# Joining the output products of two head groups, folding the value bias away, a rotary step with one addition, and new engine orders

## The chip, the cores and the metric

The kernel runs on one core of a Trainium2 chip. The core has a matrix engine (TensorE, here PE, with its weight loads shown apart as PEld), a vector engine (DVE), a scalar engine (ACT), a general engine (GpSimd, here POOL), and a queue (SyncE, here SP) that issues DMAs. They work side by side and wait for one another through semaphores; each engine takes its own instructions in the order in which the program gives them. The metric is the device time of one execution in microseconds, the median of the runs.

## The reference

Sixteen sequences of 256 tokens and 256 features go through two layers; the input of every layer step is added back to its output.

```python
x = x + attn0(cond_a(x, fside))       # cross-attention to fside, then 16 causal heads of 16 with rotary
x = x + ffn0(cond_b(x))               # matmul with a weight chosen per sequence, then FP4-quantized gated FFN
x = x + attn1(diffuse(x))             # Laplacian step, RMS norm, 16 heads of 64 in segments of 128, 16 memory tokens
x = x + moe(cond_c(x))                # gelu MLP with a chosen expert, then 8 experts, the best 2 per token
```

What the change touches in it:

```python
qkv = x @ w_qkv.T + b_qkv                         # attn0: the last third of b_qkv is the value bias
out = einsum('bhts,bhsd->bhtd', probs, v)         # rows of probs sum to 1
return out @ w_out.T + b_out
...
q = q * cos + _rotate_half(q) * sin               # attn1: rotary, k likewise
...
out = out.transpose(0, 2, 1, 3).reshape(b * w, SEG, HEADS * dh)
out = out @ W_out                                 # attn1: one product over all 16 heads
```

Everything is float32.

## The kernel before

The program has two parts. The first, `woven` (L367), does the first three lines of the reference for all sequences; the second, `mixture` (L1340), does the last. Only a little of the second (`stage_c`, L596) is pulled into the first.

In the first part the work is written as 19 stages. Each is a Python generator (`stage_a`, `stage_h`, ...) that yields one engine instruction at a time, or a condition that must hold before it goes on. The planner `weave` (L215) holds the next instruction of every stage, reckons from a table of costs (L123 to L134, `Unit.cost`) when each could start on its engine, and emits the one with the earliest start. Among those of the same engine that could start within `SLACK` of it, the rank of the stage in `ORDER` (L135) decides. So the order on each engine, SP's DMA queue included, is fixed when the program is built, by planned times and not by those of the chip. When PE's next planned start lies over `GAP` behind its last end, the planner may put in a product of the identity with itself (`kept_warm`, L394), if that fits with a `MARGIN` of 0.2 us:

```python
if best is not None and best[2][0] == "PE" and best[2][2] and best[3] > free.get("PE", 0.0) + GAP:
    op = spare()
    ...
        if max(at, ready(op, "PE")) + c[1] + MARGIN < best[3]:
```

PSUM, into which PE writes, is cut into two pairs of banks and four single banks, which the stages take in turn. Nearly every instruction of this part is recorded under L186, the line of the helper that makes it, so the profile's groups are told apart by the names of tiles.

The stages that matter here:

- `stage_a` (L439) loads the weights of the first attention (`wqkv0`, `bqkv0`, `bout0`, `wout0`) and then, for each sequence, loads `x`, adds `bout0` to it on POOL and projects queries, keys and values (`project_heads`, L663). There the biases are added on DVE, that of the values in one instruction per half sequence, `b_v<-pair,bqkv`.
- `stage_gate`, `stage_up` and `stage_down` quantize the weights of the feed-forward step at the start.
- `stage_p` and `stage_k` make queries and keys of the second attention, in 4 groups of 4 heads for each sequence, 64 groups in all. `turned4` (L1193) multiplies the projected halves by the cosines (`f_t1q`, `f_t1k`) and by the sines (`f_t2q`, `f_t2k`) on DVE, combines them by two additions on POOL, and moves the result to the layout of the scores by four DMAs (`f_q<-f_t1q`, `keys<-f_t1k`).
- `stage_s` makes the scores, `stage_g` (L1225) the exponentials. `stage_g` also issues the load of the group's 256 KB of output weights, `wo`, into one of two tiles.
- `stage_v` (L1241) calls `values4` (L1291) for each group: it transposes the probabilities (`f_prob` to `f_pT`), multiplies by the values, copies the result to `f_oT`, multiplies that by `wo` and adds the product to `x[b]` on DVE. In odd groups the memory tokens' part (`f_ppT` with `pmo`) joins the product's accumulation.

Of the kernel before, what the change touches and what calls it, by code (L numbers as in the profile page):

```python
# [13 lines left out]
F32 = mybir.dt.float32  # L14
# [97 lines left out]
class Op:  # L112
# [14 lines left out]
SIDE = {32: 0.125, 64: 0.2}  # L127
TURN = 0.01
XBUFS = 7
GAP = 0.6  # L130
MARGIN = 0.2
SLACK = {"PE": 0.0, "DVE": 0.05, "ACT": 0.1, "POOL": 0.02, "SP": 0.0}
EARLY = 200.0, 0.2
EASE = 1.5  # L134
ORDER = {  # L135
    "PE": "h y down a i m f s e g v d p gate c k x u up",
    "DVE": "d v f c h i x e a g k up gate p down u s m y",
    "ACT": "f p up h i k y gate m e a v d u g x c s down",
    "POOL": "m f h i e a y v down x g s d u up gate k p c",
    "SP": "v x a h i f p g s m d gate y u up k e c down",  # L140
}
BANK_LATER = {"PE": None, "DVE": True, "ACT": True, "POOL": None, "SP": None}


def is_ap(x):
# [293 lines left out]
def stage_a(g):  # L439
    k, a = g.k, g.a  # L440
    yield lambda: g.done["R"] == 3
    g.wqkv, op = load(g, g.w, "wqkv0", [P, 2, 3 * D], a["w_qkv0"])
    yield op
    g.bqkv, op = load(g, g.w, "bqkv0", [P, 3 * D], a["L0_attn_b_qkv"].unsqueeze(0).to_broadcast([P, 3 * D]))
    yield op
    for name in ("cos0", "sin0", "nsin0"):
        t, op = load(g, g.w, name, [P, 2, DH0 // 2], a[name])
        setattr(g, name, t)
        yield op
    g.bout, op = load(g, g.w, "bout0", [P, D], a["L0_attn_b_out"].unsqueeze(0).to_broadcast([P, D]))  # L450
    yield op
    g.wout0, op = load(g, g.w, "wout0", [P, 2, D], a["w_out0"])
    yield op


    g.done["I"] = 1
    for b in range(g.B):
        yield lambda: b < g.done["L"] + XBUFS
        x = g.x[b] = g.xp.tile([P, 2, D], F32, name="x", tag="x")
        yield g.sp.dma_start(out=x, in_=a["x"][b].rearrange("(p c) d -> p c d", p=P))  # L460
        yield lambda: g.done["B"] > b
        if b == 0:
            hT = g.first
            yield from head_constants(g)
        else:
            hT = g.a_.tile([P, 2, S], F32, name="a_h", tag="a_h", bufs=2)
            yield g.sp.dma_start(out=hT, in_=k.hd[b])
        yield g.pool.tensor_tensor(x, x, g.bout.unsqueeze(1).to_broadcast([P, 2, D]), ALU.add)
        yield lambda: g.done["M"] >= 2 * b and g.done["A"] >= b - 1
        yield from project_heads(g, b, hT)  # L470
        g.done["J"] = b + 1
# [11 lines left out]
def ahead(g, which):  # L483
# [9 lines left out]
    for b in range(which, g.B, 2):  # L493
# [7 lines left out]
        if b == 0:  # L501
            g.done["B"] += 1
            yield lambda: g.done["I"]
        else:
            yield g.sp.dma_start(out=g.k.hd[b], in_=own["e"])
            yield lambda: g.done["B"] == b
            g.done["B"] += 1


def head_constants(g):  # L510
# [152 lines left out]
def project_heads(g, b, hT):  # L663
# [4 lines left out]
    for st in range(2):  # L668
# [3 lines left out]
        yield from mm_(g, pq[:, 1, :D], [(hT[:, c, tok], g.wqkv[:, c, 2 * D : 3 * D]) for c in range(2)])  # L672
        qk = tile_a(g, 2 * D, "b_raw")
        yield g.dve.tensor_tensor(qk, pq[:, 0, :], g.bqkv[:, 0 : 2 * D], ALU.add)
        yield g.dve.tensor_tensor(v[:, st, :], pq[:, 1, :D], g.bqkv[:, 2 * D : 3 * D], ALU.add)
        g.pairs.append(pq)


# [345 lines left out]
def stage_p(g):  # L1024
# [22 lines left out]
    yield op  # L1047
    g.cos1, op = load(g, g.w, "cos1", [P, S], a["cos1"])
    yield op
    g.sin1, op = load(g, g.w, "sin1", [P, S], a["sin1"])  # L1050
    yield op

    g.pmo = g.w.tile([P, 2, D], F32, name="pmo")
    pmv = tile_l(g, [P, 2, 2, 2 * P], "wq", 2)
# [138 lines left out]
def turned4(g, zT, w, name, scale, move):  # L1193
# [3 lines left out]
    for r in range(2):  # L1197
        yield from mm_(g, pq[:, r, :], [(w[:, c, r * P : (r + 1) * P], zT[:, c, :]) for c in range(2)])
    t1, t2 = tile_l(g, [P, 2, S], f"f_t1{name}"), tile_l(g, [P, 2, S], f"f_t2{name}")
    for t, by in ((t1, g.cos1), (t2, g.sin1)):  # L1200
        table = by.unsqueeze(1).to_broadcast([P, 2, S])
        if scale is None:
            yield g.dve.tensor_tensor(t, pq, table, ALU.mult)
        else:
            yield g.dve.scalar_tensor_tensor(t, pq, scale, table, ALU.mult, ALU.mult)
    g.singles.append(one)
    yield g.pool.tensor_tensor(t1[:, 0, :], t1[:, 0, :], t2[:, 1, :], ALU.subtract)
    yield g.pool.tensor_tensor(t1[:, 1, :], t1[:, 1, :], t2[:, 0, :], ALU.add)
    for a in range(2):
        for r in range(2):  # L1210
            yield move(slice(r, P, 2), a, t1[64 * a : 64 * a + 64, r, :])
# [13 lines left out]
def stage_g(g):  # L1225

    for i in range(4 * g.B):
        yield lambda: (i, 0) in g.scored and g.done["V"] > i - 2
        wo = tile_l(g, [P, 2, D], "wo", 2)
        yield g.sp.dma_start(out=wo, in_=g.a["w_out1"][:, 2 * (i % 4) : 2 * (i % 4) + 2, :])  # L1230
        if i % 2 == 0:
            g.pm = tile_l(g, [P, 2, 8, PM], "f_pm", 2)
        prob = [None, None]
        g.live[i] = prob, g.pm, wo
        for st in range(2):
            yield lambda: (i, st) in g.scored
            prob[st] = yield from exponentials4(g, i % 4, st, *g.scored.pop((i, st)))
# [50 lines left out]
    return prob  # L1288


def values4(g, n, b, v, prob, pm, wo):  # L1291

    pT = []
    for st in range(2):
        yield lambda: g.done["G"] > 2 * (4 * b + n) + st
# [17 lines left out]
    oT = tile_l(g, [P, 2, S], "f_oT", 2)  # L1313
    yield copy_(g, twined(oT), untwined(po))
    g.singles.append(one)
    if n % 2 == 1:
        ppT = tile_l(g, [P, S], "f_ppT")
        one = yield from single(g, pm)
        pt = one[:, :S]
        for st in range(2):  # L1320
            yield g.pe.transpose(pt[:, st * P : (st + 1) * P], pm[:, st].rearrange("p j n -> p (j n)"), g.ident)
        rows = lambda t: t.unsqueeze(1)
        yield copy_(g, twined(rows(ppT)), untwined(rows(pt)))
        g.singles.append(one)
    one = yield from single(g, oT)
    pp = one.rearrange("p (s d) -> p s d", s=2)
    for st in range(2):
        tok = slice(st * P, (st + 1) * P)
        pairs = [(oT[:, c, tok], wo[:, c, :]) for c in range(2)]
        if n % 2 == 1:  # L1330
            pairs.append((ppT[:, tok], g.pmo[:, n // 2, :]))
        yield from mm_(g, pp[:, st, :], pairs)
    yield g.dve.tensor_tensor(g.x[b], g.x[b], pp, ALU.add)
    g.singles.append(one)
# [509 lines left out]
```

## Time and profile before

| | |
|---|---|
| runs | 2491.32 us median of 3 (2489.93 to 2493.8) |
| profiled execution | 2491.22 us, of which span 2489.5 us |
| planner-ordered part | about 0 to 1516 us of the span |
| expert part | about 1516 us to the end |
| granted PE clock, mean | 0.999 |
| PE busy | 2447.2 us, 98% |
| DVE, ACT, POOL busy | 1345.4, 1205.1, 1061.1 us |

The profile is one execution. Times are counted from the first instruction. A group line names engine, operation, the tile written and the tiles read, the shape (partitions x elements) and the count; then the busy time in us, the mean duration of one in ns, and the idle time of the engine before these instructions with what ended it. A PE line begins with the rows and columns of the stationary operand. A float32 product appears as two PE records; a transpose as one. A waits line says who waited for whom, in total us, how often, and the longest.

### The profile page before, as it was taken

The page shows a single profiled execution, that of the slowest core. Times are in us where ns is not written, and L with a number is a line of the kernel's source. Part 1 is how long each engine was busy: PE and PEld are TensorE (multiplying, and loading weights), DVE is VectorE, ACT ScalarE, POOL GpSimd, SP SyncE. Part 2 cuts the span into 40 slices and gives each one's busy share as a digit, 9 for nine tenths or more (in the row PEclk, how much of TensorE's full clock was granted, in tenths as well). Part 3 has the DMA queues.
Part 4 walks back from the last instruction along what each step waited for, and adds up shares of the span by engine and source line. Part 5 has one row for each costly group of instructions (what it writes and reads, how often), then busy time and mean ns, then how long its engine had stood idle before and what let it go on. Part 6 is the DMA issues. An engine that isn't in the chain of part 4 may idle for free. (4 is left out here: it accounts for less than half of the span.)

```text
span 2489.5 us, 39426 instructions
## 1 busy us (share of the span) xinstructions
PE 2447.2 (98%) x13339; PEld 1859.7 (75%) x13339; DVE 1345.4 (54%) x2640; ACT 1205.1 (48%) x3567; POOL 1061.1 (43%) x1212
## 2 busy tenths in 40 slices
PE   8999999999999999999999999999999999999999
PEld 7776777777777777777778885555668888888866
DVE  6777877978888877888876652333300000000023
ACT  3765666666676666666664554223212322322311
POOL 6555666666666656675665442333200000000044
PEclk9999999999999999999999999999999999999999
DMA  5432332322233232222233544111224556555433
GB/s 163 145 128 80 96 103 68 100 92 73 87 93 99 73 96 83 79 88 88 83 100 118 174 136 141 51 51 51 79 81 153 198 181 201 199 185 198 155 101 108
DMA packets 229725, 285.00 MB, mean 114 GB/s; under 512 B 45233, under 2 KB 192657, under 8 KB 220177
## 3 DMA queue, kind: packets, MB, share of 16 engines
q1 hardware_dynamic: 223376, 265.66, 33.7%
q0 software_dynamic: 6144, 16.79, 2.1%
q8 instruction: 108, 1.77, 0.3%
q14 instruction: 97, 0.79, 0.1%
HBM read 210.78 MB, written 33.82 MB: 98 GB/s over the span
## 5 line engine op out<-in xcount | busy, mean ns | idle before, releaser
L1472 POOL DMA_INDIRECT got<-osort,pos_o x64 | 62.0, 968 | 628.5 <-ACT hT L1405 585.6
L1454 ACT ACTIVATE ehT<-bank,own_b 128x256 f32<-128x256 f32 x280 | 132.5, 473 | 349.1 <-PE bank L53 349.1
L53 PE MATMUL bank<-ysT,w 128*128 128x256 f32 x1120 | 247.5, 379 | 0.2 <-ACT ysT L108 0.2
L53 PE MATMUL bank<-w,ehT 128*128 128x256 f32 x1120 | 247.5, 379 | 0.0
L186 PE MATMUL single<-e_zT,wq 128*128 128x256 f32 x1024 | 243.6, 381 | 1.8 <-DMA wq<-in_w_qk 1.0
L53 PEld LDWEIGHTS bank<-ysT,w 128*128 128x128 f32 x1120 | 212.7, 190 | 29.4 <-ACT ysT L108 0.5
L53 PEld LDWEIGHTS bank<-w,ehT 128*128 128x128 f32 x1120 | 210.2, 190 | 27.2
L186 POOL TENSOR_TENSOR b_e<-b_e,b_stat 128x1024 f32<-128x1024 f32 x124 | 186.1, 1502 | 104.2 <-DVE b_stat L186 87.4
L186 ACT ACTIVATE b_e<-b_e,b_stat 128x256 f32<-128x256 f32 x496 | 220.4, 448 | 12.8 <-DVE b_stat L186 12.7
L186 ACT ACTIVATE f_prob<-f_prob,f_stat 128x144 f32<-128x144 f32 x512 | 207.6, 409 | 24.7 <-DVE f_stat L186 24.5
L186 PEld LDWEIGHTS single<-e_zT,wq 128*128 128x128 f32 x1024 | 185.7, 190 | 26.4 <-issue 2.0
L186 POOL TENSOR_TENSOR f_prob<-f_prob,f_stat 128x512 f32<-128x512 f32 x128 | 136.1, 1063 | 110.6 <-DVE f_stat L186 98.3
L1462 DVE TENSOR_TENSOR eo<-bank,eb 128x512 f32<-128x512 f32 x35 | 24.2, 692 | 234.4 <-PE bank L53 234.4
L186 ACT COPY b_pT<-single 128x512 f32<-128x512 f32 x186 | 108.2, 586 | 68.2 <-PE single L186 67.6
L1569 POOL DMA_INDIRECT ysort<-r_y,r_posi x64 | 62.4, 976 | 162.9 <-DMA ysort<-r_y,r_posi 101.7
L186 PE MATMUL single<-wo,f_oT 128*128 128x256 f32 x512 | 128.2, 383 | 0.5 <-ACT f_oT L186 0.4
L1421 DVE COPY own_b<-b1t 128x8 f32<-128x8 f32 x35 | 5.9, 174 | 222.3 <-ACT ehT L1454 222.3
L186 PE MATMUL single<-wv,e_zT 128*128 128x256 f32 x512 | 121.9, 381 | 0.0
L1405 ACT ACTIVATE hT<-bank,b 128x512 f32<-128x512 f32 x64 | 43.9, 687 | 157.4 <-PE bank L53 151.2
L186 POOL TENSOR_TENSOR f_t1q<-f_t1q,f_t2q 128x256 f32<-128x256 f32 x128 | 99.3, 791 | 41.6 <-DVE f_t2q L186 20.4
L186 PE MATMUL single<-ident,b_e 128*128 128x128 f32 x744 | 113.0, 277 | 3.4 <-POOL b_e L186 1.2
L186 DVE TENSOR_REDUCE b_stat<-b_e 128x4 f32<-128x1024 f32 (+1 forms) x124 | 114.5, 941 | 1.4 <-ACT b_e L186 0.8
(329 smaller groups left out, 5406.4 us busy)
## 6 DMA issues: line engine op xcount, KB each, us to landing
w<-in_w SPq DMA_DIRECT2D x70, 1024.0 KB
wq<-in_w_qk SPq DMA_DIRECT2D x128, 256.0 KB
wv<-in_w_v SPq DMA_DIRECT2D x64, 256.0 KB
keys<-f_t1k SPq DMA_DIRECT2D x256, 64.0 KB
f_q<-f_t1q SPq DMA_DIRECT2D x256, 64.0 KB
wo<-in_w_out SPq DMA_DIRECT2D x64, 256.0 KB
ys<-ysort SPq DMA_DIRECT2D x35, 256.0 KB
osort<-eo SPq DMA_DIRECT2D x35, 256.0 KB
```

What stands on the lines that cost most here:

```text
L53: nc.tensor.matmul(out, lhsT, rhs, start=start and i == 0, stop=stop and i == last)
L186: return Op([(self.name, self.cost(fn, outs, aps), lambda: call(*args, **kw))], outs, aps)
L1405: nc.scalar.activation(hT[:, f, :], ph, AF.Gelu_apprx_tanh, bias=k.b1[:, NE, f : f + 1])
L1421: nc.vector.tensor_copy(b1, r.b1t[:, t, :])
L1454: nc.scalar.activation(hT[:, f, :], ph, AF.Gelu_apprx_tanh, bias=b1[:, f : f + 1])
L1462: nc.vector.tensor_tensor(o, po, b2.unsqueeze(1).to_broadcast([P, 2, D]), ALU.add)
L1472: nc.gpsimd.indirect_dma_start(out=g, out_offset=None, in_=k.osort[:, :], in_offset=bass.IndirectOffsetOnAxis(ap=r.pos_o[:, i, t : t + 1], ...
L1569: nc.gpsimd.indirect_dma_start(out=k.ysort[:, :], out_offset=bass.IndirectOffsetOnAxis(ap=posi[:, i, t : t + 1], axis=0), in_=ys[t], in_of ...
```

## The change

Four things are done at once.

- Output products: `values4` now issues the load of `wo` itself, at its head. An even group stops after `f_oT` and keeps `f_oT` and `wo`; the odd group that follows multiplies both groups' in one accumulation, with the memory tokens' part, and one addition to `x[b]` serves two groups.
- Value bias: a new function `output_bias` is called once in `stage_a` before the loop over sequences. It transposes the value bias, multiplies it by `wout0` and adds the product to `bout0`; this is the same sum, since the rows of the probabilities add up to 1. The values are copied out of PSUM by `copy_`, which lets the planner choose ACT or DVE.
- Rotary: the table of sines gets two rows, the first negated on POOL once; DVE reads the two halves in PSUM in swapped order, and a single POOL addition over 512 elements takes the place of two over 256.
- Orders: the ranks in `ORDER` are other ones for all five engines, and `GAP` is 0.3 in place of 0.6. `BANK_LATER` for PE becomes `True`; no PE instruction reads PSUM, so the term that it switches stays zero.

```diff
-GAP = 0.6
+GAP = 0.3
...
-    "PE": "h y down a i m f s e g v d p gate c k x u up",
-    "DVE": "d v f c h i x e a g k up gate p down u s m y",
-    "ACT": "f p up h i k y gate m e a v d u g x c s down",
-    "POOL": "m f h i e a y v down x g s d u up gate k p c",
-    "SP": "v x a h i f p g s m d gate y u up k e c down",
+    "PE": "h y down g a m i f s e v d gate p k u c x up",
+    "DVE": "d x v f c h i e a g k up gate down p s u m y",
+    "ACT": "up f p k h i y gate m e a d u v g c x s down",
+    "POOL": "e m f h i a y v down x g s d u up gate k p c",
+    "SP": "v x a h i g f p s m gate y u d up k e c down",
...
+    yield from output_bias(g)
     for b in range(g.B):
...
+def output_bias(g):
+    t = g.a_.tile([P, 2, P], F32, name="bvT", tag="b_raw")
+    one = yield from single(g, g.bqkv)
+    pt = one.rearrange("p (c t) -> p c t", t=P)
+    for c in range(2):
+        yield g.pe.transpose(pt[:, c, :], g.bqkv[:, 2 * D + c * P : 2 * D + (c + 1) * P], g.ident)
+    yield copy_(g, t, pt[:, :2, :])
+    g.singles.append(one)
+    one = yield from single(g, t)
+    yield from mm_(g, one[:, :D], [(t[:, c, :], g.wout0[:, c, :]) for c in range(2)])
+    yield g.dve.tensor_tensor(g.bout, g.bout, one[:, :D], ALU.add)
+    g.singles.append(one)
...
-        yield g.dve.tensor_tensor(v[:, st, :], pq[:, 1, :D], g.bqkv[:, 2 * D : 3 * D], ALU.add)
+        yield copy_(g, v[:, st, :], pq[:, 1, :D])
...
-    g.sin1, op = load(g, g.w, "sin1", [P, S], a["sin1"])
-    yield op
+    g.sin2 = g.w.tile([P, 2, S], F32, name="sin2")
+    yield g.sp.dma_start(out=g.sin2[:, 1, :], in_=a["sin1"])
+    yield g.pool.tensor_scalar(g.sin2[:, 0, :], g.sin2[:, 1, :], -1.0, None, ALU.mult)
...
-    for t, by in ((t1, g.cos1), (t2, g.sin1)):
-        table = by.unsqueeze(1).to_broadcast([P, 2, S])
+    for t, by, src in ((t1, g.cos1.unsqueeze(1).to_broadcast([P, 2, S]), pq), (t2, g.sin2, pq[:, ::-1, :])):
...
-    yield g.pool.tensor_tensor(t1[:, 0, :], t1[:, 0, :], t2[:, 1, :], ALU.subtract)
-    yield g.pool.tensor_tensor(t1[:, 1, :], t1[:, 1, :], t2[:, 0, :], ALU.add)
+    yield g.pool.tensor_tensor(t1, t1, t2, ALU.add)
...
-        wo = tile_l(g, [P, 2, D], "wo", 2)
-        yield g.sp.dma_start(out=wo, in_=g.a["w_out1"][:, 2 * (i % 4) : 2 * (i % 4) + 2, :])
...
-def values4(g, n, b, v, prob, pm, wo):
+def values4(g, n, b, v, prob, pm):
+    wo = tile_l(g, [P, 2, D], "wo", 2)
+    yield g.sp.dma_start(out=wo, in_=g.a["w_out1"][:, 2 * n : 2 * n + 2, :])
...
+    if n % 2 == 0:
+        g.even = oT, wo
+        return
...
-        pairs = [(oT[:, c, tok], wo[:, c, :]) for c in range(2)]
-        if n % 2 == 1:
-            pairs.append((ppT[:, tok], g.pmo[:, n // 2, :]))
+        pairs = [(o[:, c, tok], w[:, c, :]) for o, w in (g.even, (oT, wo)) for c in range(2)]
+        pairs.append((ppT[:, tok], g.pmo[:, n // 2, :]))
         yield from mm_(g, pp[:, st, :], pairs)
```

## The prediction

> **What bounds the kernel now.** I read the page's engine totals first, then busy time by stretch, then the groups of TensorE (PE) in a stretch, then what PE waited for, and last the rows of the operations that are edited.
>
> ```profile
> span 2489.5 us, 39426 instructions
> PE 2447.2 (98%) x13339; PEld 1859.7 (75%) x13339; DVE 1345.4 (54%) x2640; ACT 1205.1 (48%) x3567; POOL 1061.1 (43%) x1212
> PEclk9999999999999999999999999999999999999999
> ```
>
> PE is busy 98% of the span at full clock, no other engine above 54%. The profiled execution took 2491.22 us, 1.7 us around a span of 2489.5; the median of the runs is 2491.32. I sum against 2491.2.
>
> The planner-ordered part ends at about 1516 us, where the code of `mixture`, which the change leaves alone, begins. So I cut the span at 300, 1350 and 1516 us. Columns: stretch, its length, busy time of PE, weight loads, DVE, ACT, POOL, then clock and DMA.
>
> ```profile
> 0.00:300.00 300.00, 282.09 (x1720) 217.95 (x1721) 222.73 (x403) 175.02 (x547) 169.05 (x186) 1.00 0.39 123
> 300.00:1350.00 1050.00, 1038.17 (x6525) 781.03 (x6524) 844.92 (x1472) 683.98 (x2257) 673.03 (x764) 1.00 0.30 89
> 1350.00:1516.00 166.00, 164.10 (x1072) 132.86 (x1071) 88.99 (x160) 86.30 (x293) 74.35 (x111) 1.00 0.44 131
> 1516.00:2489.00 973.00, 962.79 (x4027) 727.82 (x4025) 188.81 (x610) 259.82 (x470) 144.66 (x152) 1.00 0.41 136
> ```
>
> PE idles 17.9 us in the first stretch, 11.8 in the second, 1.9 in the third. Busy PE is not all useful: the planner fills expected gaps with products of the identity with itself (`kept_warm`). They are the group that reads the identity alone; here for 0 to 300 us, then 300 to 1350, then 1350 to 1520.
>
> ```profile
> L186 PE MATMUL single<-ident 128*128 128x128 f32 x368 | 50.2, 284 | 1.7 <-POOL ident masks.py:199 1.6 <-DVE f_t2k L186 0.2
> ...
> L186 PE MATMUL single<-ident 128*128 128x128 f32 x4 | 1.0, 326 | 0.0
> ...
> L186 PE MATMUL single<-ident 128*128 128x128 f32 x28 | 4.6, 293 | 0.0
> ```
>
> So what can be won is 17.9 + 50.2 = 68 us at the start, 11.8 + 1.0 = 13 in the middle and 1.9 + 4.6 = 6.5 near its end, 87 us in all. The rest is PE at work, which the change does not shorten. In the middle PE waits in small pieces, for chains through POOL, DVE and ACT:
>
> ```profile
> PE single L186 <- POOL d_h L186: 1.7, 4, 0.6
> PE pair L186 <- POOL b_diag L186: 1.3, 4, 0.4
> PE single L186 <- DVE x L186: 1.2, 1, 1.2
> PE single L186 <- POOL b_qk L186: 1.1, 1, 1.1
> ```
>
> **The change part by part.** These rows price it (count, busy us, mean ns):
>
> ```profile
> L186 DVE TENSOR_TENSOR x<-x,single 128x512 f32<-128x512 f32 x80 | 54.4, 680 | 47.9 <-PE single L186 47.4
> L186 DVE TENSOR_TENSOR b_v<-pair,bqkv 128x256 f32<-128x256 f32 x32 | 13.1, 410 | 0.0
> L186 ACT COPY f_ppT<-single 128x256 f32<-128x256 f32 x32 | 12.0, 375 | 6.9 <-PE single L186 6.8
> L186 POOL TENSOR_TENSOR f_t1q<-f_t1q,f_t2q 128x256 f32<-128x256 f32 x128 | 99.3, 791 | 41.6 <-DVE f_t2q L186 20.4 <-DVE f_stat L186 12.1 <-issue 7.3
> L186 POOL TENSOR_TENSOR b_qk<-b_t,b_t 128x512 f32<-128x512 f32 x32 | 41.0, 1283 | 37.9 <-DVE b_t L186 26.4 <-DVE f_stat L186 9.3 <-DVE b_stat L186 1.5
> L186 POOL TENSOR_TENSOR f_prob<-f_prob,f_stat 128x512 f32<-128x512 f32 x128 | 136.1, 1063 | 110.6 <-DVE f_stat L186 98.3 <-PE single L186 10.9 <-DVE b_stat L186 0.3
> ```
>
> Output products. Two groups now add up in one PSUM bank. The products stay the same in number and size; 32 of the 80 additions to `x` go: 32 x 0.680 = 21.8 us of DVE, and 32 bank holdings. All of it lies beside PE.
>
> Value bias. 32 additions (13.1 us of DVE) become copies, which the planner may give to ACT at 0.375 each, 12 us there. Once, at the start: two transposes, a copy, two products and one addition to `bout0`. Transposes start 0.109 us apart and 256-wide records 0.216 apart, two records to a float32 product, so PE gets 2 x 0.109 + 4 x 0.216 = 1.1 us. It falls among the identity products after 13 us, so 0 on PE. If that cover is gone, 1.1. Its addition of 0.41 and perhaps its copy join a DVE that works on the weights' chain from 18 to 26 us, and PE waits 2.1 us for that chain at 23 us: between 0 and 1.1 us, I take 0.5. Behind it in its stage stand the load of `x[0]`, the constants on POOL (23.0 us) and the first projection (24.2). The loads before and with `wout0` add up to 3.35 MB, at the 226 GB/s of the first 25 us some 15 us after the first at 2.7. So the bias is done near 20 us, my estimate, and they do not wait.
>
> Rotary step. Two POOL additions of 0.79 (1.58 together) become one of 128x512, which the trace has not in this place: between 1.06 (`f_prob`, one operand a broadcast) and 1.33 (`x` + `bout`). I take 1.28 from `b_qk`, likewise two full tiles. 128 x 0.30 = 38 us of POOL, beside PE; the sine table's negation takes some 0.8 back, once. DVE reads the PSUM halves swapped and a two-row table, as many elements as before: 0.68 stays, at worst 0.83 as for the SBUF row `e_near` (128 x 0.15 = 19 us of DVE); I take 0. The moves of the first half could start after the first addition (at 1125.10, when POOL had begun at 1124.35); now all four wait 1.28 instead of 0.79, so SP's queue behind them is held 0.5 us longer per step. PE waits for none of these DMAs in the trace, so 0; with that cover gone it would be 128 x 0.5 = 64 us.
>
> Output weights. Their DMA, 64 times, moves from the softmax stage to the head of `values4`, so it leaves that place in SP's queue and stands ahead of the group's transposes instead. An even group's weights are needed a group later; their tile, one of two, is free once the odd product before has read it, so SP's queue, with the moves of `q` and `k` behind, can stand there for PE, as it did when the load sat in the softmax stage. An odd group's must land between its first transposes and its product.
>
> ```profile
> SPq L186 <- POOL f_t1q L186: 225.5, 74, 12.5
> SPq L186 <- POOL f_t1k L186: 213.3, 67, 13.1
> ```
>
> In SP's own waits, the queue stands for POOL up to 13.1 us, 3 us on average. The first weights were issued at 231.4 us for a product at 266.6. From first transposes to first product of an odd group I count, by start times in the timeline, 5.4 us at least and 14.5 in the median. A 256 KB load at 89 GB/s (the middle's mean rate, so a lower bound of speed) takes 2.9 us; with 3 us of queue it fits, with 13 it does not. I take 0; the range holds +1 us for each of 32 groups.
>
> The Trainium skill ("DMA: Bandwidth & Descriptors", Rules for kernel authors) says to issue a DMA early and wait for it late, which speaks against this move. By its fixed 2.0 us (Anatomy of one DMA, given for the gpsimd path) I estimate the load at some 5 us instead of 2.9, which still fits the median; no wait here shows the figure.
>
> Orders and gap. Every engine's order is set anew, and the identity product is now put in from gaps of 0.416 us (its planned 0.216 plus the margin of 0.2) instead of 0.6. PE's clock is 1.00 in every stretch already, and its longest wait for a releaser is 2.2 us, so more filling cannot raise the clock. One product costs 0.22 us where the gap was not there; with 184 now (368 records), 20 to 60 more cost 0 to 13 us if all missed, and I take 0 as they sit where PE would wait.
>
> The skill ("TensorE: Matmul & The Clock Gate", Why this matters for your kernels) asks only that no gap exceeds some 3 us. Agreed by the 2.2 us above; by that rule the smaller gap is worth nothing and can only cost.
>
> What the order is worth no row shows. It can move only the 87 us. At the start much is latency: the first loads, the weights' quantization, the first attention; 37 of the 50 us of filling lie before 110 us. I bound it there by a third won (-23) and by 15 us lost, and take -5. Relief on DVE and POOL adds -2 there, near 200 to 300 us where rotary begins. In the middle DVE loses 24 x 0.68 + 24 x 0.41 = 26 us of 845, POOL 96 x 0.30 = 29 of 673; of the 13 us of PE's loss I take a third, -4 (0 to -6). Near the end -1 (0 to -3).
>
> Sum: +0.5 - 5 - 2 - 4 - 1 = -11.5, so 2491.2 - 11.5 = 2479.7, say 2480. The ends of the likeliest case: -31 (2460) and -5 (2486).
>
> **The rivals.** (A) Hidden anyway: the start is bound by loads and chains that no order moves, and PE's small waits return behind other producers. For it: DVE and POOL are not the bound anywhere (80% and 64% in the middle). Against: 50 us of filling say that PE was short of ready work. Time 2486 to 2496. (B) Slower, by the order alone: priorities fitted to the planner's durations put a PE instruction ahead whose input comes later on the chip than planned, and PE takes its instructions in turn. Place: the first 300 us, where PE waits some 2 us for POOL's weights twice already. Ten such waits of 2 us cost 20, 2511; it decides once they exceed the 11.5 won, so from six on. Against: in the middle PE idles 1.1%, so plan and chip agree well. (C) Slower, by late output weights: 32 x 1 us = +32, less 11.5, so 2512; it decides where the average hold passes 0.36 us.
>
> **How the numbers follow.** Forecast 0.60, A 0.16, B 0.19, C 0.05. About 5 us (0.2%) is what a measurement tells from no change: faster 0.60, same 0.16, slower 0.24. The time is the likeliest case's, whose own range is 2460 to 2486. Over all cases 2460 to 2504 leaves out about 0.05 below and 0.13 above (the worse half of B and C).
>
> **What would show it.** Right: `x` additions of 512 fall from 80 to 48, no `b_v` addition, 128 POOL rotary additions near 1.28 us instead of 256; the stretch to 1516 ends about 12 us earlier, mostly by fewer identity products and less idle before 300 us; the part after it keeps 973 us. Wrong: PE waiting for DMA of the output weights (C), identity products or PE idle before 300 us above 68 us together (B), or POOL's addition above 1.58 us.

## The result and the profile after

The change made the kernel slower: 2525.7 us in the median (2522.71 to 2527.54) against 2492.56 us for the kernel before on the same chip, a ratio of 1.0131 with a 95% interval of 1.0114 to 1.0149. The prediction was 2480 us with a range of 2460 to 2504, so it had the wrong direction and the time lies outside its range. The profiled execution took 2527.54 us, with a span of 2525.8 us. The ratios here and below are those of fast runs; one execution of `edits_only`, 7186.29 us, was none and stands only in that run's median.

The engine totals of the page of after:

```profile
span 2525.8 us, 39290 instructions
PE 2474.4 (98%) x13463; PEld 1881.7 (74%) x13463; DVE 1325.2 (52%) x2578; ACT 1214.1 (48%) x3599; POOL 1032.1 (41%) x1085
```

DVE has 20.2 us less to do than before and POOL 29.0 less, and still the span is 36.3 us longer. PE looks as busy as it was, 98%, and is busy 27 us longer.

The busy time by stretch, after, with the columns of the prediction (stretch, its length, PE, weight loads, DVE, ACT, POOL, clock, DMA). The last product of the planner-ordered part ended at 1524.2 us before and ends at 1561.9 us now, so I cut there:

```profile
0.00:300.00 300.00, 288.43 (x1762) 225.71 (x1764) 209.52 (x377) 170.96 (x530) 163.31 (x170) 0.99 0.38 120
300.00:1350.00 1050.00, 1022.74 (x6380) 766.10 (x6379) 811.45 (x1393) 680.50 (x2264) 631.79 (x652) 0.99 0.30 87
1350.00:1561.90 211.90, 210.37 (x1318) 166.12 (x1316) 116.71 (x204) 105.10 (x343) 93.65 (x128) 1.00 0.42 123
```

All of the loss is in the ordered part: 1561.9 - 1524.2 = 37.7 us, while what follows takes 964 us, where it took 965. PE idles 11.6 us up to 300 us, where it was 17.9, but 27.3 us in the middle, where it was 11.8, and the clock is 0.99 in both stretches, where it was 1.00. The identity products of after, in 0 to 300, 300 to 1350 and 1350 to 1562 us:

```profile
L186 PE MATMUL single<-ident 128*128 128x128 f32 x466 | 63.2, 285 | 2.0 <-POOL ident masks.py:199 1.6 <-DVE b_pT L186 0.2 <-ACT e_zT L186 0.2
...
L186 PE MATMUL single<-ident 128*128 128x128 f32 x4 | 0.6, 274 | 0.0
...
L186 PE MATMUL single<-ident 128*128 128x128 f32 x48 | 7.3, 286 | 0.0
```

They take 71.1 us where they took 55.8. That gives a balance of the 37.7 us: 15.3 more of identity products, 8.8 more of idle time (11.6 + 27.3 + 1.5 = 40.4 against 17.9 + 11.8 + 1.9 = 31.6), some 1.1 for the products of the value bias, and at most 8.5 lost to the clock, which is worked out below; at least 4 us are not placed. The first 300 us have little of it: identity products and idle time come to 74.8 us there, where they were 68.1.

The edited operations, after:

```profile
L186 DVE TENSOR_TENSOR x<-x,single 128x512 f32<-128x512 f32 x48 | 32.7, 681 | 51.4 <-PE single L186 51.4
...
L186 ACT COPY b_v<-pair 128x256 f32<-128x256 f32 x32 | 11.9, 373 | 43.8 <-DVE b_raw L186 43.8
...
L186 POOL TENSOR_TENSOR f_t1q<-f_t1q,f_t2q 128x512 f32<-128x512 f32 x64 | 85.6, 1337 | 47.1 <-DVE f_stat L186 18.8 <-DVE f_t2q L186 14.9 <-issue 5.9
L186 POOL TENSOR_TENSOR f_t1k<-f_t1k,f_t2k 128x512 f32<-128x512 f32 x64 | 84.2, 1316 | 47.7 <-DVE f_t2k L186 22.6 <-DVE f_stat L186 12.4 <-issue 11.9
```

Each edit did to its own operations what it was expected to do. The time went elsewhere, and three places can be looked at.

**The start.** PE's timeline, after: the transposes of the value bias, its products with `wout0`, and the first projection of the first attention.

```profile
24.97 0.38 PE L186 MATMUL single<-ident,bqkv 128*128 128x128 f32 x2
...
26.75 1.03 PE L186 MATMUL single<-wout,bvT 128*128 128x256 f32 x4
...
40.59 1.88 PE L186 MATMUL pair<-wqkv,a_h 128*128 128x512 f32 x4
```

The same projection in PE's timeline of before:

```profile
24.16 1.88 PE L186 MATMUL pair<-wqkv,a_h 128*128 128x512 f32 x4
```

The load of `x[0]` in SP's timeline of before:

```profile
13.42 0.43 SPq L186 DMA_DIRECT2D x<-in_x  x1
```

The same load in SP's timeline of after:

```profile
27.01 0.43 SPq L186 DMA_DIRECT2D x<-in_x  x1
```

The bias was done only at 28 us. What stands behind it in `stage_a` waited for it: the load of `x[0]` by 13.6 us, the first projection by 16.4. How much PE lost by it is another matter. The 6.7 us that the first 300 us lost are no measure of it: `orders_only` below, which has no bias, has 59.9 us of identity products and 13.8 us of idle time there, 5.6 us more than before. The first product with `wo` begins at 304.3 us instead of 266.6, but the joined products put it off as well: `merge_alone` below, whose first projection begins at 25.2 us, has it at 304.0.

**The middle.** PE's longest waits, after:

```profile
PE single L186 <- POOL d_h L186: 6.1, 7, 2.0
PE single L186 <- DVE d_h L186: 4.8, 3, 3.7
PE pair L186 <- DMA keys<-f_t1k: 4.4, 5, 1.7
PE single L186 <- POOL c_y L186: 3.1, 4, 1.5
PE pair L186 <- DVE f_prob L186: 2.9, 2, 2.2
```

Before, the first was 3.3 us and the fifth 0.3, and PE waited neither for DVE's `d_h` nor for keys. The wait of 3.7 us can be followed back through the timeline of after around it:

```profile
802.09 0.37 SPq L186 DMA_DIRECT2D wc<-in_cat_w  x1
...
803.26 0.35 SPq L186 DMA_DIRECT2D bc<-in_L_cond_b  x1
...
803.66 0.55 SPq L186 DMA_DIRECT2D e_near<-x  x1
...
806.61 0.72 POOL L186 TENSOR_TENSOR e_near<-e_near,x 128x256 f32<-128x256 f32 x1 [4.58 <-DMA e_near<-x]
...
807.37 1.51 DVE L186 SCALAR_TENSOR_TENSOR e_u<-e_near,condB_zY,e_u 128x512 f32<-128x512 f32 x1 [2.94 <-POOL e_near L186]
...
809.47 0.50 DVE L186 SCALAR_TENSOR_TENSOR d_h<-d_th,single 128x352 f32<-128x352 f32 x1
...
810.02 0.96 PE L186 MATMUL single<-gateT,c_yT 128*128 128x352 f32 x1 [3.74 <-DVE d_h L186]
```

Read from below: PE stands for `d_h`, which DVE could not make because it takes its instructions in turn and stood at `e_u`; that waited for POOL's `e_near`, and that for a load which SP issued behind two others, `wc` and `bc` of `stage_y`. In the new ranks of SP, the Laplacian step (`stage_d`) stands behind `m gate y u`. POOL's waits for these loads, before and after (total us, times, longest):

```profile
POOL e_near L186 <- DMA e_near<-x: 8.9, 7, 2.7
...
POOL e_near L186 <- DMA e_near<-x: 25.8, 13, 6.0
```

**The clock.** Three stretches of after's busy time by stretch, around the stalls:

```profile
139.60:143.00 3.40, 1.67 (x13) 1.10 (x12) 3.36 (x4) 2.63 (x10) 2.71 (x3) 1.00 0.65 227
143.00:146.40 3.40, 3.40 (x11) 2.87 (x11) 0.91 (x3) 0.00 (x0) 2.34 (x4) 0.51 0.62 180
...
805.20:808.60 3.40, 1.09 (x7) 0.59 (x5) 1.23 (x1) 0.07 (x1) 1.72 (x2) 1.00 0.06 18
808.60:812.00 3.40, 1.98 (x4) 1.23 (x5) 3.35 (x7) 2.19 (x9) 2.85 (x4) 0.51 0.00 0
812.00:815.40 3.40, 3.40 (x14) 1.36 (x12) 3.06 (x3) 1.85 (x6) 2.67 (x3) 0.50 0.09 24
...
1221.70:1225.10 3.40, 1.27 (x7) 0.51 (x6) 3.40 (x8) 0.91 (x4) 2.58 (x2) 1.00 0.16 54
1225.10:1231.90 6.80, 6.75 (x22) 5.28 (x23) 6.78 (x12) 3.06 (x11) 4.99 (x7) 0.50 0.19 45
```

The third column from the end is the clock, 1.00 and then 0.50. After 3.4 us in which PE was busy for 1.1 to 1.7 us, it ran at half speed for 3.4 or 6.8 us. In all that is 17 us at half speed up to 1562 us, of which at most 8.5 us are lost; for part of them PE stood anyway, as from 808.6 to 812.0 us. Before, there was no such stretch in the ordered part.

### The profile page after: what moved, and what is told of

Read it like the earlier page. It is cut to its first block, busy times and chain, and to the rows that moved or that the text cites. A ratio compares the mean times of both kernels' runs of the same rounds, so it can differ in the third digit from the quotient of the medians.

```text
span 2525.8 us, 39290 instructions
## 1 busy us (share of the span) xinstructions
PE 2474.4 (98%) x13463; PEld 1881.7 (74%) x13463; DVE 1325.2 (52%) x2578; ACT 1214.1 (48%) x3599; POOL 1032.1 (41%) x1085
## 5 line engine op out<-in xcount | busy, mean ns | idle before, releaser
L1479 DVE TENSOR_TENSOR eo<-bank,eb 128x512 f32<-128x512 f32 x35 | 24.2, 692 | 234.4 <-PE bank L53 234.4
L186 PE MATMUL single<-wo,f_oT 128*128 128x256 f32 x512 | 122.3, 381 | 0.0
L53 PE MATMUL bank<-yT,w1s 128*128 128x512 f32 x256 | 111.6, 593 | 1.6 <-DVEq L1395 1.6
```

The lines of the kernel that those rows point to most:

```text
L53: nc.tensor.matmul(out, lhsT, rhs, start=start and i == 0, stop=stop and i == last)
L186: return Op([(self.name, self.cost(fn, outs, aps), lambda: call(*args, **kw))], outs, aps)
L1479: nc.vector.tensor_tensor(o, po, b2.unsqueeze(1).to_broadcast([P, 2, D]), ALU.add)
```

## The experiments

The first theory after the result was that the orders are the loss: every change of an instruction or of a rank makes the planner set all orders anew, and the orders of before fitted its operations better than a new set does. The rivals were the edits themselves: the bias at the start, the later moves of the rotary step, the joined products, and the identity products.

The planner reckons a time for each instruction as the program is built. In the table "reckoned" is the end of the last PE instruction of the ordered part by that reckoning, which is no measurement, "trace" is the same instruction's end in the trace, and the lag is the difference. Times are medians; the ratio is to the kernel before on the same chip.

| kernel | time us | ratio (95%) | reckoned | trace | lag |
|---|---|---|---|---|---|
| before | 2491.2 to 2493.6 | | 1508.7 | 1524.2 | 15 |
| after | 2525.7 | 1.0131 (1.0114, 1.0149) | 1518.5 | 1561.9 | 43 |
| orders_only | 2506.76 | 1.0062 (1.0045, 1.0078) | 1514.8 | 1540.9 | 26 |
| hop_051 | 2505.39 | 1.0056 (1.0039, 1.0072) | 1515.9 | 1539.7 | 24 |
| hop_049 | 2492.33 | 1.0001 (0.9991, 1.0010) | 1510.4 | 1525.4 | 15 |
| gap_alone | 2493.72 | 1.0006 (0.9996, 1.0016) | 1508.7 | 1527.5 | 19 |
| rot_in_old_order | 2492.16 | 1.0002 (0.9993, 1.0012) | 1508.7 | 1527.2 | 18 |
| rot_alone | 2507.69 | 1.0067 (1.0049, 1.0085) | 1510.9 | 1537.6 | 27 |
| bias_alone | 2516.7 | 1.0093 (1.0076, 1.0109) | 1520.2 | 1553.5 | 33 |
| merge_alone | 2517.18 | 1.0092 (1.0074, 1.0110) | 1527.3 | 1555.7 | 28 |
| edits_only | 2538.24 | 1.0188 (1.0168, 1.0209) | 1527.4 | 1572.8 | 45 |
| bias_after_first | 2515.36 | 1.0090 (1.0073, 1.0107) | 1507.7 | 1550.7 | 43 |
| addition_priced | 2510.74 | 1.0068 (1.0050, 1.0086) | 1504.4 | 1544.7 | 40 |
| priced_odd_early | 2501.85 | 1.0037 (1.0023, 1.0051) | 1499.2 | 1538.1 | 39 |
| shift_loads_first | 2516.8 | 1.0099 (1.0082, 1.0116) | 1521.7 | 1552.4 | 31 |
| halves_in_new_order | 2518.34 | 1.0104 (1.0087, 1.0121) | 1518.5 | 1552.2 | 34 |
| measured_prices | 2488.07 | 0.9986 (0.9977, 0.9996) | 1513.1 | 1524.7 | 12 |
| ranks_for_edits | 2475.05 | 0.9931 (0.9917, 0.9944) | 1506.3 | 1510.7 | 4 |
| ranks_rot_bias | 2479.26 | 0.9949 (0.9933, 0.9964) | 1507.3 | 1513.8 | 7 |
| ranks_no_edit | 2482.61 | 0.9960 (0.9945, 0.9976) | 1517.9 | 1518.0 | 0 |

**The change taken apart.** `orders_only` is the kernel before with `GAP`, `ORDER` and `BANK_LATER` of after; `edits_only` is the kernel after with those of before.

> The kernel before with the new orders and gap, none of the three edits. Three theories. Orders: the new ranks bring the loss of 33 us, so about 2520 to 2530. Edits: the joined products, the bias and the rotary step bring it, so 2487 to 2498. Re-plan: the old schedule was a lucky one among many alike, and whatever makes the planner plan anew loses. The planner's own planned end of PE's part, which the program works out as it is built, is 1508.7 us before, 1518.5 after the change and 1514.8 here; re-plan expects at least those 6 us, and up to 20 more where the chip falls behind the plan: 2498 to 2520.

> All three edits with the old orders and the old gap. Orders: no loss, 2480 to 2497. Edits: the whole loss, 2520 to 2530. Re-plan: the planned end is 1527.4 us here, 18.7 later than before, so 2511 at least, up to 2535; then the new orders would have won some of it back.

The orders alone cost 16 us on the old operations, as the theory of re-planning expected, and the edits with the old ranks cost 47, which is 3 us above the highest of the three ranges expected. The kernel after lies between: its ranks are 14 us better for its operations than the old ranks are (33 against 47), and worse for the old operations.

**The same work in other orders.**

```diff
-HOP = 0.05
+HOP = 0.051
```

> The kernel before with one constant of the planner's cost table moved by a thousandth of a us (HOP 0.05 to 0.051): the same instructions, the same work, the same ranks. Orders and edits both expect 2490 to 2496, since neither is touched. Re-plan: the planned end moves from 1508.7 to 1515.9, so 2498 to 2515 for no change of the work at all.

```diff
-HOP = 0.05
+HOP = 0.049
```

> The kernel before, same work and ranks; only the planner's time from one engine to another is 0.049 us in place of 0.05, as in hop_051, with the other sign. Theory 'order': any setting anew of all the orders loses what the one of before was picked for, 2495 to 2510. Rival 'hop_051 was a mishap, the orders are worth little': 2488 to 2495.

No instruction differs in either, only the planner's time from one engine to another, by 1 ns. `hop_051` lost 14 us: its orders are others from some 60 us on, to the end. The planner reckoned 7 of the 14 itself (1515.9 for 1508.7). `hop_049` lost nothing, and missed the expectation, but it tells little: its orders on all engines are those of before up to about 1296 us. So a full new set of orders can cost 14 us by itself, as `hop_051` and, with other ranks, `orders_only` show.

**The gap.**

```diff
-GAP = 0.6
+GAP = 0.3
```

> The kernel before with the gap alone at 0.3 in place of 0.6, so that identity products are put in at shorter planned gaps. Theory 'order': they sit where PE would wait, within 4 us of before, 2487 to 2496. Rival 'the fillers take PE's time': some 45 more products of 0.22 us, up to 10 us slower, 2497 to 2502.

There are 90 more records of identity products in the ordered part (490 for 400), and no difference in time that can be measured.

**The rotary step, with orders held.** `rot_in_old_order` is the kernel before in which every instruction keeps its place, and the two POOL additions become one in the place of the second. DVE reads the halves swapped as in after, and the negated sines come with the load:

```diff
-    yield g.pool.tensor_tensor(t1[:, 0, :], t1[:, 0, :], t2[:, 1, :], ALU.subtract)
-    yield g.pool.tensor_tensor(t1[:, 1, :], t1[:, 1, :], t2[:, 0, :], ALU.add)
+    yield in_place(g.pool.tensor_tensor(t1[:, 0, :], t1[:, 0, :], t2[:, 1, :], ALU.subtract), lambda: None)
+    yield in_place(
+        g.pool.tensor_tensor(t1[:, 1, :], t1[:, 1, :], t2[:, 0, :], ALU.add),
+        partial(g.k.nc.gpsimd.tensor_tensor, t1, t1, t2, ALU.add),
+    )
```

> The kernel before, with every engine's order held as it was: each instruction stands where it stood, only the first of the two POOL additions of the rotary step is left out, the second becomes the one addition over 512 elements, and the sine table has two rows (its negated half comes from the host with the load). Theory 'order': the operations themselves cost nothing, the loss lies in orders that fit worse, so 2485 to 2496. Rival 'lost head start': the moves of the first half now wait for the whole addition, 0.5 us longer in 128 steps, and PE stands for keys and scores; 5 to 20 us slower than before, 2497 to 2512.

`halves_in_new_order` is the reverse, the kernel after with its orders held and the addition issued as two:

```diff
-    yield g.pool.tensor_tensor(t1, t1, t2, ALU.add)
+    yield halves(g, t1, t2)
```

> The kernel after, with every engine's order held as it is: only the one POOL addition of the rotary step is issued as two additions of its halves. Theory 'order': no gain, as POOL works 0.3 us longer in each of 128 steps and the orders stay; 2522 to 2535. Rival 'lost head start': the moves of the first half go 0.5 us earlier again, PE's 4.4 us of waits for keys and DVE's 8.0 us go; 5 to 15 us faster than after, 2511 to 2521.

In the old order the single addition costs nothing and gains nothing that the times show, within 3 us either way: POOL's groups in `rot_in_old_order` show the same operation at the same price as in after, and the 26 us of POOL saved there (99.3 + 98.7 - 171.6) lie beside PE.

```profile
L269 POOL TENSOR_TENSOR f_t1k<-f_t1k,f_t2k 128x512 f32<-128x512 f32 x64 | 86.5, 1352 | 27.5 <-DVE f_t2k L269 20.9 <-issue 5.0 <-POOL f_pm L186 1.1
L269 POOL TENSOR_TENSOR f_t1q<-f_t1q,f_t2q 128x512 f32<-128x512 f32 x64 | 85.1, 1329 | 23.6 <-DVE f_t2q L269 20.8 <-issue 1.1 <-POOL f_pm L186 1.0
```

In the new order, giving the first half back its head start gained about 7 us, with slightly more POOL work. PE's waits for keys in `halves_in_new_order`:

```profile
PE pair L186 <- DMA keys<-f_t1k: 3.0, 3, 1.5
```

They were 4.4 us in 5 times. In the two profiled executions, some 5 us of the 7 are the clock: 6.8 us at half speed in place of 17, as the stretches at 143 and 1225 us are gone, that at 808 is half as long, and one at 923 is new. The time lies in the range of the rival, the lost head start. So the same 0.5 us is free in one order and, as far as this shows, not in another; the two intervals overlap a little, so the size of this gain is not sharp.

**The loads of the Laplacian step.** The kernel after with `d` further ahead on SP:

```diff
-    "SP": "v x a h i g f p s m gate y u d up k e c down",
+    "SP": "v x a h i g f p s m d gate y u up k e c down",
```

> The changed kernel with one rank moved back: on SP the diffusion stage (its six shift loads e_near) stands ahead of the gate, y and u stages again. In the changed kernel PE stands 3.7 us at 810 us and 2.2 us at 1225 us behind DVE instructions that wait for these loads through POOL, and the granted clock is 0.5 for 6.8 us after each. If the rank on SP causes those, both go, with 6 us of idle time and 7 us of half clock: 2510 to 2516. Re-plan: the planned end is 1521.7, 3.2 later, and the stalls may return elsewhere: 2515 to 2540.

Some 8 us came back (25.6 us above before instead of 33.1), though the planner set the orders anew and reckoned 3 us more. PE's longest wait for DVE's `d_h` is 0.7 us there, for `f_prob` 1.1, and the stretches at half speed at 809 and 1225 us are gone (one of 3.4 us at 918 is new). That the rank of `d` did this is not shown. The time is 0.8 us above the range of the theory and within that of the rival, all orders are new ones, and POOL's waits for the loads are fewer by only 3.5 us, though the longest is half as long:

```profile
POOL e_near L186 <- DMA e_near<-x: 22.3, 15, 3.3
```

Nor does this rank alone set them: they are 15.0 us in `orders_only`, which has after's rank, and 45.3 us in `edits_only`, which has that of before.

**The place of the value bias.** `bias_after_first` is `edits_only` with the bias folded in behind the first projection:

```diff
-    yield from output_bias(g)
     for b in range(g.B):
...
-        yield g.pool.tensor_tensor(x, x, g.bout.unsqueeze(1).to_broadcast([P, 2, D]), ALU.add)
+        if b:
+            yield g.pool.tensor_tensor(x, x, g.bout.unsqueeze(1).to_broadcast([P, 2, D]), ALU.add)
...
         yield from project_heads(g, b, hT)
+        if not b:
+            yield from output_bias(g)
+            yield g.pool.tensor_tensor(x, x, g.bout.unsqueeze(1).to_broadcast([P, 2, D]), ALU.add)
```

> All three edits with the ranks and gap of before, as in edits_only (2538.24), but the value bias is folded in after the first sequence's projection and not ahead of the load of its x. Theory 'bias stands in the way at the start': the first projection goes back from 40.6 to about 24 us, PE's useful lag at 100 us and what follows from it go; 2490 to 2515. Rival 'the place of the bias is nothing, other steps of the edits are the loss': 2530 to 2545.

The first projection goes back to where it was, and the bias follows. PE's timeline of `bias_after_first`:

```profile
24.62 2.75 PE L186 MATMUL pair<-wqkv,a_h 128*128 128x512 f32 x8
29.87 2.75 PE L186 MATMUL pair<-wqkv,a_h 128*128 128x512 f32 x8
34.64 0.38 PE L186 MATMUL single<-ident,bqkv 128*128 128x128 f32 x2
36.48 1.13 PE L186 MATMUL single<-wout,bvT 128*128 128x256 f32 x4
```

It gained 23 of the 47 us and came out 0.4 us beyond the slow end of what the theory expected (2515), so something else of that size remained. The start is where it was; that all 23 us come from it is argued, since every order was set anew here too.

**One edit alone**, with the ranks of before; each is its hunks of the change's diff.

> The kernel before with the rotary edit alone; the planner sets the orders anew with the old ranks. Theory 'new orders': the operation itself cost nothing with the orders held, so all that shows is what the orders lose, 2495 to 2512. Rival 'the rotary edit is free': 2487 to 2495.

> The kernel before with the value bias folded in ahead of the first sequence, alone, with the old ranks. Theory 'bias stands in the way at the start': the first projection at about 40 us instead of 24 and 10 to 25 us slower, 2501 to 2517. Rival 'it costs only together with the other edits': 2487 to 2500.

> The kernel before with the output products of two groups joined, alone, the load of the output weights at the head of values4, with the old ranks. Theory 'the place of the weights' load and the new orders cost': 5 to 25 us slower, 2496 to 2516. Rival 'free': 2487 to 2496.

All three lost, 16, 25 and 26 us. For the rotary step the comparison with `rot_in_old_order` is clean but for the one negation of the sines on POOL: the operation costs 0, the orders that the planner makes for it cost 16. For the bias the first projection began at 38.9 us, the delay again; no run holds the other orders and moves the bias alone, so how much of the 25 us is the delay stays open. For the joined products no run holds the orders, so it is open how much of the 26 us is theirs (the time is 1 us above the theory's range); no wait of PE for a load of their weights appears in its trace, but five stretches of 3.4 us at half speed do, and five in that of `bias_alone`. The three sum to 67 us, more than the 47 of the edits together, so these losses do not add up like costs of operations.

**The planner's prices.** What makes a new set of orders worse? In the table the slow kernels lag 24 to 45 us behind the planner's reckoning, and before lags 15. The planner prices an instruction on POOL by

```python
COSTS = {"DVE": (0.15, 0.00105), "ACT": (0.16, 0.00083), "POOL": (0.30, 0.0016)}
```

so an addition over 512 elements at 0.30 + 512 x 0.0016 = 1.12 us, whereas after's groups above show 1.32 to 1.34. `addition_priced` corrects this one price in `bias_after_first`:

```diff
-    yield g.pool.tensor_tensor(t1, t1, t2, ALU.add)
+    op = g.pool.tensor_tensor(t1, t1, t2, ALU.add)
+    op.choices = [("POOL", 1.3, op.choices[0][2])]
+    yield op
```

> bias_after_first (2515.36) with one number more: the planner reckons the one POOL addition of the rotary step at 1.3 us, as the chip takes it (1.37 and 1.30 there), in place of its own 1.12. Theory 'price': 128 additions that end 0.2 us later than planned put the moves, the keys and PE's products behind the plan, so 8 to 25 us go, 2490 to 2507. Rival 'any new plan is as good as any other, the loss of 23 us has no single cause': 2508 to 2525.

`priced_odd_early` also loads the odd group's output weights in the softmax stage, with `"POOL": (0.302, 0.0016)`:

```diff
+        wo = None
+        if i % 2:
+            wo = tile_l(g, [P, 2, D], "wo", 2)
+            yield g.sp.dma_start(out=wo, in_=g.a["w_out1"][:, 2 * (i % 4) : 2 * (i % 4) + 2, :])
```

> addition_priced with two edits more: the output weights of the odd group are loaded in the softmax stage as before, those of the even group at the head of values4, and the planner's fixed part of a POOL instruction is 0.302 in place of 0.30, which sets the orders anew once more. Theory 'price and place of the bias': all three edits then cost nothing and this plan can show their gain, 2478 to 2500. Rival 'any new plan loses 10 to 25 us': 2501 to 2520.

Both fell on the rival's side, the first by 4 us and the second by 2. One price is not it: the lag stayed at 40 and 39 us. The reckoned ends fell to 1504.4 and 1499.2, so the planner's reckoning, as it was, is a poor guide to the time on the chip.

`measured_prices` is `priced_odd_early` with the prices of 39 kinds of instruction multiplied to the means that the trace of `bias_after_first` shows (among them `b_t` on DVE, 0.71 us for a price of 0.53, and `e_near` on POOL, 0.94 for 0.71). It takes 0.6 us for an SP issue, has other ranks, set for these prices, and `EASE`, the planner's surcharge on DVE for work that ACT could do, at 2.0 for 1.5:

```diff
-            return Op([(self.name, self.cost(fn, outs, aps), lambda: call(*args, **kw))], outs, aps)
+            key = (self.name, plain(outs[0]), tuple(sorted({plain(x) for x in aps})))
+            cost = self.cost(fn, outs, aps) * MEASURED.get(key, 1.0)
+            return Op([(self.name, cost, lambda: call(*args, **kw))], outs, aps)
```

> All three edits as in priced_odd_early (2501.85), with the planner's prices of 39 kinds of instruction multiplied to what the traces of bias_after_first show, an SP issue reckoned at 0.6 us, and ranks set for these prices. Theory 'price': chip and plan stay together, PE's waits of the middle go, 2475 to 2492. Rival 'the prices are not it': 2495 to 2520.

The lag fell from 39 to 12 us, and with all three edits in it the kernel is 0.1% faster than before. Prices and ranks changed together, so no run says which of them did it.

**Versions that beat both.** With these prices, other ranks and small constants of the planner (`GAP` 0.45; for `ranks_no_edit` also `HOP` 0.06 and `EARLY` from 100 us) were chosen for all three edits, for all but the joined products, and for none. The ranks of `ranks_for_edits`, which has the weights' load at the head of `values4` as the change has it, but the value bias behind the first projection:

```diff
+    "PE": "h y g a i m f s e down v d p gate c k x u up",
+    "DVE": "v d c h x i e a p f g k up gate down u s m y",
+    "ACT": "f p up h i k y down gate m e v a d u g x c s",
+    "POOL": "m f h i e a y v down x g s u d up gate p k c",
+    "SP": "x a h i f p d g v s m gate u e y up c k down",
```

> All three edits, the value bias after the first projection, the weights' load at the head of values4, prices as in measured_prices, and ranks chosen for them. Theory 'price and ranks': the plan is kept on the chip, 2476 to 2487, faster than before. Rival 'the edits themselves cost': 2490 to 2510.

> As ranks_for_edits without the joined output products, with ranks chosen for it. Theory 'price and ranks': 2477 to 2488, within 4 us of ranks_for_edits, as the joined products take nothing from PE. Rival 'the joined products are a gain or a loss of their own': more than 6 us away from ranks_for_edits.

> The kernel before without any of the edits, with the measured prices and ranks chosen for it. Theory 'the edits are worth little beside the ranks': 2482 to 2498, within 12 us of ranks_for_edits. Rival 'relief of DVE and POOL is the gain': 2500 or more.

All three beat the kernel before, and `ranks_for_edits` beats it by 0.69% (0.56% to 0.83%), 1 us more than expected. So the edits, with the bias in its later place, are no loss in themselves. `ranks_rot_bias` lies 4.2 us behind it. The busy time by stretch of `ranks_for_edits`, and its longest waits of PE:

```profile
0.00:300.00 300.00, 290.92 (x1779) 226.43 (x1780) 225.74 (x396) 184.25 (x577) 174.91 (x182) 1.00 0.40 127
300.00:1350.00 1050.00, 1043.75 (x6561) 787.95 (x6561) 842.39 (x1429) 686.53 (x2284) 654.21 (x672) 1.00 0.31 90
1350.00:1510.70 160.70, 160.59 (x1024) 126.69 (x1022) 81.65 (x145) 83.25 (x275) 66.39 (x95) 1.00 0.44 129
```

```profile
PE single L238 <- POOL d_h L238: 2.3, 4, 1.2
PE single L238 <- DVE e_zT L238: 2.0, 2, 1.4
```

PE idles 15.4 us in the ordered part, where it was 31.6 before and 40.4 after, and the clock is 1.00 throughout. The ordered part ends at 1510.7 us, 13.5 earlier than before. POOL's single addition takes 1.32 to 1.39 us there in the mean.

The kernel without any edit, with ranks of its own, gained too (0.40%). It lies 7.6 us behind `ranks_for_edits`. Whether that is the relief of DVE and POOL or better luck with the ranks is not settled: the ranks were chosen for each separately, and the runs above show that ranks alone move the time by 14 us. It is also open which of the 39 prices matters.

## Why the prediction was wrong, step by step

- **What bounds the kernel** was right: PE, with the loss in idle pieces and identity products before 1524 us. The bound of 87 us held for what can be won, but it was read as if nothing could be lost beyond 15 us.
- **Output products**: the sizes were right (48 additions of 0.681 us, 32 gone). "I take 0" for the load of the weights holds in after, where PE's waits show none for `wo`; rival C did not happen.
- **Value bias**: a second step that failed is "the bias is done near 20 us ... and they do not wait". It was taken from the bandwidth of the loads. It was done at 28 us, and the first projection went from 24.2 to 40.6 us. What the term of +0.5 us should have been stays open: with the old ranks its place was worth 23 us in `bias_after_first`, and alone the edit cost 25, both with all orders set anew; in after the first 300 us lost only 6.7 us in idle time and identity products, and `orders_only`, without the bias, lost 5.6 there.
- **Rotary step**: 1.28 us was the median (1.277), and the mean of 1.33 left 28 us of relief instead of 38. The swapped reading on DVE cost nothing (0.675 us before and after), as taken. "PE waits for none of these DMAs in the trace, so 0" is true in the old order, where the run gives 1.0002, and failed in the new one, where PE waited 4.4 us for keys and two half additions gave back about 7 us. The cover that hid it was a property of the order, and the order was replaced.
- **Gap**: 0 was right (1.0006, within the interval of no change).
- **Orders**: this is the step that failed first. -12 in sum was the largest term and had no row. They cost +16 on the old operations, and new orders cost 14 with no work changed at all. What failed is that the trace of before was read to price only gains, and that edits and orders were summed as if apart. In the middle, where a third of PE's loss of 13 us was to be won, PE idled 27.3 us instead of 11.8. Rival B named the mechanism, a PE instruction put ahead whose input comes later than planned. By the test given for it, identity products and idle above 68 us before 300 us, it is met with 63.2 + 11.6 = 74.8; but those 7 us are no waits: PE idled less there than before and had 13.0 us more of identity products, and the waits that B meant lie in the middle. Its argument against, "plan and chip agree well" since PE idled only 1.1%, judged the old orders, not the new ones.
- **Clock**: "more filling cannot raise the clock" was right, and the other side was left out: stalls can lower it. That cost at most 8.5 us. The trace of before had shown it once, in the expert part, by a wait shorter than the 2.2 us that were read as agreeing with the skill's rule (last section).
- **The sum** was short of its own bounds: 23 + 2 + 6 + 3 us at best make -34, not -31. Nothing hangs on it.
- **The forecast of 2480** is near what the edits reach with ranks that fit them (2475.05). This doesn't make it right: the change on trial brought other ranks and another place of the bias.

## What to carry to other kernels

Where a planner fixes the order of five engines, an edit's cost is not the cost of its operations: hold the order and change the operation alone (`rot_in_old_order`: 0), then change the order alone (`hop_051`: 14 us), before crediting either. An instruction that yields ahead of a loop holds all that the loop would have started, so ask which load it waits for, not how long it runs. Compare the plan with the trace before trusting it: by the old prices `priced_odd_early` was to end 9.5 us earlier than before (1499.2 against 1508.7) and ran 10 us longer, while the kernels with measured prices and ranks chosen for them kept to their plan within 12 us and were faster.

## What the runs showed of the hardware

PE's clock halved for 3.4 or 6.8 us at a time after stalls that were mostly shorter than that. In after the longest idle pieces were 1.34, 3.74 and 2.18 us long, within 3.4 us in which PE was busy 1.67, 1.09 and 1.27 us in all. The starts of the halved stretches are multiples of 3.413 us apart: from 143.0 to 808.6 us it is 195 times, from 808.6 to 1225.1 us 122 times. So a stall's cost depends on how it falls: the kernel before waited 2.07 us just ahead of 23.0 us without losing the clock, and PE was busy 1.99 and 2.52 us in the two stretches of 3.4 us that share this wait (from 18.92 and 22.33 us). In its expert part it waited 1.97 us ahead of 2372.9 us, was busy 1.44 us from 2370.7 to 2374.1, and then ran at half speed for 3.4 us. Where the line lies is not sharp: 1.80 us busy was too little in `hop_051` (from 51.3 us), and 1.48 us was enough in `bias_after_first` (from 19.9 us). The Trainium skill ("TensorE: Matmul & The Clock Gate", What's actually happening) describes a free-running window of 3413 ns, and the traces agree with it. Its advice ("Why this matters for your kernels"), no gaps over some 3 us, is too mild for these runs, where a wait of 1.34 us beside smaller ones was enough once. How the stretches fall differs between runs of one program: the four of `rot_alone` took 2505.54, 2505.32, 2509.84 and 2512.96 us at mean clocks of 0.999, 0.998, 0.997 and 0.996. A profile shows one of them, so a gain in clock between two profiles, as with `halves_in_new_order`, can be chance in part.

Instructions of one shape on DVE with two SBUF operands differ widely: the 64 of `b_t<-b_raw,cos_qk` over 256 elements took 0.43 us in the median and 0.71 in the mean in `bias_after_first`, while `f_t2q`, which reads PSUM, keeps within a few per cent. No run here tells the cause; a fixed price for such an instruction cannot be right either way.
